# Two cross-attention layers on one core: ScalarE copies the values' bank, and a new order of scores, maxima and turns

## The chip, the core and the metric

The kernel runs on one core of a Trainium2 chip, as one program. The metric is the device time of that core in microseconds (us); the number compared is the median over several runs. A core has TensorE (PE; its weight loads are listed as PEld), VectorE (DVE), ScalarE (ACT), GpSimd (POOL) and SyncE (SP), which here only issues DMAs. The engines run side by side, each works through its own instructions strictly in order, and they meet at semaphores. Matmul results land in PSUM, which has eight banks of 128 partitions by 512 float32.

## The reference

Two cross-attention layers follow each other on x (32 batches, 256 positions, 320 channels; 20 heads of 16). Both attend to one context of 32 x 77 x 512. Layer 0 splits its context into 77 text rows and three more parts, and layer 1 into 77 text rows and a rest; the context has 77 rows, so the text part is all there is, and the other softmaxes are over nothing.

```python
q = _heads(x @ to_q_w)                       # 32 x 20 x 256 x 16
k, v = _heads(ctx @ to_k_w), _heads(ctx @ to_v_w)
s = jnp.einsum('bhqd,bhkd->bhqk', q, k) / np.sqrt(16)
p = jax.nn.softmax(s, axis=-1)               # over 77 keys
out = _merge(jnp.einsum('bhqk,bhkd->bhqd', p, v))
x = out @ to_out_w + to_out_b + x            # then layer 1 in the same way, with its own weights
```

## The kernel before

**Units.** A unit is two batches (one pair `p`) in one layer; 16 pairs and 2 layers make 32 units `u`, in an order that runs layer 0 four pairs ahead of layer 1. x lies as channels by positions: 320 channels are 128 + 128 + 64, and two batches' 64 rest channels share one 128-partition tile. So a unit has five *groups* `g` of 128 channel rows by 256 positions (groups 0 to 3: two channel blocks by two batches; group 4: the rest of both batches). A group holds eight heads, in four pairs, one for each quarter of 32 partitions.

**Steps of a unit.** `queries` or `outputs_and_queries` make the queries, and ScalarE copies them to SBUF. `keys` and `keys_rest` make the keys; ScalarE copies them (`kR`), and GpSimd masks them by head parity (`kT`). `split_keys` and `split_queries` split both on GpSimd into a rounded half and the difference (`k_halves`, `halves`), and DMAs on SP spread these over partitions. `vals` makes the context's values (`psv`), which ScalarE copies to `stage` and a DMA places in `v`. Per group there are then these steps:

- `maxima` (L500, L512): for one *half* of a group (128 positions) four matmuls, one for each quarter of 32 partitions, write scores with positions on partitions into four banks `psm`; two or three halves lie side by side in each bank, and VectorE reduces every bank to row maxima.
- `turn(u)` (L532 to L537), once per unit: VectorE rounds the maxima, subtracts, transposes, and four DMAs on SP lay them as rows into `max_rows`.
- `scores` (L550, L558): four banks `pss`; four matmuls write minus the maxima over all 512 columns, sixteen add the products; ScalarE takes four exponentials to `pT` (L564).
- `values` (L578 to L605): sixteen matmuls write one bank `po` with values and sums (128 x 512); VectorE transposes it in blocks of 32 to `turned` (L590) and takes the reciprocal of the sums (L594); GpSimd multiplies to `normal` (L599).
- `turn_back` (L613): VectorE transposes `normal` into the unit's `oT`, 256 columns per group.
- `finish`, or in a running kernel `outputs_and_queries`: the output matmuls of unit u - 3 (`psy`, from `oT`) and the queries of unit u (`psq`), with VectorE's additions of bias and residual (L620) in between. `main_channels` takes group 0, 1, 2, 3 of `oT` in this order, four matmuls each; the 64-row matmuls that take group 4 come after 64 + 16 others.

**Banks.** All PSUM tiles are one rotating tag of eight banks: every new bank waits until the bank eight allocations before it has been read. The order of the steps thus decides which engine's read a block of matmuls waits for.

**Order.** The framework's scheduler is switched off (`tc.manual_schedule()`). Steps are put by `at(slot, where, step)` into slots, and each slot is issued as written, one kind of step after another. The main part has slots 0 to 134, and four units fill a cycle of 17 slots. By the slot's number in its cycle:

| slot of the cycle | scores | maxima | values | else |
|---|---|---|---|---|
| 0 | 1 group | 3 halves | 1 group | turn, turn back, outputs and queries |
| 1, 2 | 1 | 3 halves | 1 | context values; in 1 keys |
| 3, 4 | 1 | 2 halves | 1 | keys; in 4 turn |
| 5, 9, 13 | 2 groups | none | 1 | outputs and queries |
| 6, 10, 14 | 1 | 3 halves | 2 groups | keys, context values; in 10 and 14 turn |
| 7, 11, 15 | 1 | 3 halves | 1 | two turn backs, keys, mostly context values |
| 8, 12, 16 | 1 | 3 halves | 1 | keys |

The values of a group come one slot after its scores, and groups 0 to 3 are turned back one slot after their values, group 4 in the same slot. Each kind of engine work follows this order, also on VectorE, GpSimd, ScalarE and SP. The order within a slot is

```python
rest = ("values", "rest", "back", "turn", "split", "full", "last")
if slot > 0 and work_of[slot] > 10 * S:
    order = ("load", "scores", "turn back", "maxima") + rest
else:
    order = ("load", "maxima", "turn back", "scores") + rest
```

where `work_of` counts columns of projections and values put into the slot. By it, 88 of the 135 slots have scores first: the output slots (0, 5, 9, 13), the slots with context values, and most of the end. Keys are placed in "rest", outputs and queries in "full", the turn back of group 4 in "back". Of the slots with maxima first, 31 have three halves (slots 1 to 4 of the first cycle, all slots 8, 12 and 16, five slots 2, and slot 113).

Of the kernel before, what the change touches and what calls it, by code (L numbers as in the profile page):

```python
# [52 lines left out]
F32 = mybir.dt.float32  # L53
# [42 lines left out]
def xattn_kernel(ctx: ExitStack, tc: tile.TileContext, xT, cT, cP, weights, outT):  # L96
# [24 lines left out]

    def load_context(u):
        p = units[u][0]
        c_sb = cs[u] = io.tile([P, NKA, NB * L], F32, tag="c", name=f"c_{u}", bufs=3)
        nc.sync.dma_start(out=c_sb, in_=cP[:, p])


# [23 lines left out]

    ones = const.tile([P, P], F32, name="ones")
    nc.vector.memset(ones, 1.0)
    ident = const.tile([P, P], F32, name="ident")
    make_identity(nc, ident)


# [364 lines left out]
    def turn(u):  # L522

        assert u < 2 or (u - 2, NG - 1) in scored
        m = st[u].pop("m").rearrange("p e (g c) j -> p e g (c j)", c=2)
        to = maxes.rearrange("p t y x -> p t (y x)")
        to = to.rearrange("p t (e w g i) -> p t i e g w", e=2, w=8, i=2)
        for t in range(2):
            n = 4 - 3 * t
            new = m[:, :, 4 * t : 4 * t + n]  # L530
            high, low = (to[:, t, i, :, 0:n] for i in range(2))
            nc.vector.tensor_copy(high.bitcast(F32R), new)  # L532
            nc.vector.tensor_tensor(low, new, high, ALU.subtract)  # L533
        mT = work.tile([P, 2 * 4 * 32], F32, tag="mT", name=f"mT_{u}", bufs=1)
        nc.vector.transpose(mT, maxes.rearrange("p t y i -> p (t y i)"))
        for a in range(4):
            nc.sync.dma_start(  # L537
                out=max_rows[u % 2].bitcast(F32).rearrange(
                    "(r x) t (y a n) -> x a r (t y) n", x=4, a=4, n=32
                )[0, a],  # L540
                in_=mT[32 * a : 32 * a + 32].rearrange("r (y n) -> r y n", n=32),
            )


    def scores(u, g):
        scored.add((u, g))
        ps = [bank(f"pss_{u}_{g}_{j}") for j in range(4)]
        for j in range(4):
            r = slice(32 * j, 32 * j + 32)
            nc.tensor.matmul(  # L550
                ps[j][:L], less[r, g % 4, :], max_rows[u % 2][r, g // 4], start=True, stop=False
            )
        for e in range(2):
            q = of_group(st[u]["qs"][:, e], g)
            for half in range(2):
                for j in range(4):
                    r = slice(32 * j, 32 * j + 32)
                    nc.tensor.matmul(  # L558
                        ps[j][:L, e * S : (e + 1) * S], st[u]["ks"][r, e, g, half, :], q[r, :],
                        start=False, stop=(half == 1 and e == 1),  # L560
                    )
        st[u]["p", g] = [probs.tile([P, 512], F32, tag="pT", name=f"pT_{u}_{g}_{j}") for j in range(4)]
        for j in range(4):
            nc.scalar.activation(st[u]["p", g][j][:L], ps[j][:L], AF.Exp, scale=SCALE)  # L564
# [19 lines left out]
                )  # L584
        return po

    def divide(u, g, po):

        turned = work.tile([P, 2 * (S + HD)], F32, tag="turned", name=f"turned_{u}_{g}", bufs=2)
        nc.vector.transpose(turned[:, 0 : 2 * S], po)  # L590

        sums = turned[:, HD : 2 * S - HD].rearrange("p (e n) -> p e n", e=2)[:, :, 0 : S - HD : 32]
        inv = work.tile([P, 2, S // 32], F32, tag="inv", name=f"inv_{u}_{g}", bufs=2)
        nc.vector.reciprocal(inv, sums)  # L594

        outs = turned.rearrange("p (e n) -> p e n", e=2)[:, :, 0:S]
        outs = outs.rearrange("p e (q r) -> p e q r", r=32)[:, :, :, 0:HD]
        normal = work.tile([P, S // 32, 2, HD], F32, tag="normal", name=f"normal_{u}_{g}", bufs=2)
        nc.gpsimd.tensor_tensor(  # L599
            normal.rearrange("p q e d -> p e q d"),  # L600
            outs,
            inv.unsqueeze(3).broadcast_to([P, 2, S // 32, HD]),
            ALU.mult,
        )
        return normal  # L605

    def values(u, g):
        st[u]["n", g] = divide(u, g, products(u, g))

    def turn_back(u, g):  # L610

# [41 lines left out]

    place = {}

    work_of = {}

    def at(slot, where, step, columns=0):

        place.setdefault((slot, where), []).append(step)  # L660
        work_of[slot] = work_of.get(slot, 0) + columns

    def start(u):

# [15 lines left out]
        NU - 2: (end - 2, end - 1, end - 2),  # L680
    }
    made = [0, 0]
    for u, (p, layer) in enumerate(units):

        s = start(u - 2)
        if layer == 0 and u > 0:
            at(s - 5 - (u == 1), "load", lambda p=p: load_x(p))
        if u > 0:
            at(s - 4, "load", lambda u=u: load_context(u))
        if u > 1:  # L690
            k = (0, 1, 2) if u == 2 else (s - 2, s - 1, s + 1)
            at(k[0], "rest", lambda u=u: keys(u, 0), 8 * 2 * L)
            at(k[1], "rest", lambda u=u: keys(u, 1), 8 * 2 * L)
            at(k[2], "rest", lambda u=u: keys_rest(u), 8 * L)
        paired = u > 2 and u - 3 not in late
        if paired:
            at(s, "full", lambda u=u: outputs_and_queries(u - 3, u), 50 * S)
        elif u > 1:
            at(s, "last", lambda u=u: queries(u), 25 * S)
        if u > 1:  # L700
            at(s + 2, "split", lambda u=u: split_keys(u))
            at(start(u - 1), "load", lambda u=u: spread_keys(u))
            for i in range(3):
                at(start(u - 1) + i - 1, "split", lambda u=u, i=i: split_queries(u, i))
                at(start(u - 1) + i, "load", lambda u=u, i=i: spread_queries(u, i))
        need = range(p * NB * L // P, ((p + 1) * NB * L - 1) // P + 1)
        new = [i for i in need if i >= made[layer]]
        made[layer] += len(new)
        first = (-6, -2)[u] if u < 2 else start(u - 1) + 1
        slots = {}  # L710
        for k, i in enumerate(new):
            at(first - 3 - (u == 0) + k, "load", lambda layer=layer, i=i: load_chunk(layer, i))
            if i in few:
                slots[i] = first
                at(first, "full", lambda layer=layer, i=i: vals_of_few(layer, i), 8 * 96)
                continue
            for h in range(2):
                slots[i] = first + (0 if u < 2 else k if len(new) > 1 else h)
                at(slots[i], "full", lambda layer=layer, i=i, h=h: vals(layer, i, h), 4 * C)
        for i in need:  # L720
            at(slots.get(i, first), "full", lambda u=u, i=i: place_vals(u, i))
        for g in range(NG):
            slot = slot_of(u, g)
            at(slot, "scores", lambda u=u, g=g: scores(u, g))
            at(slot + 1, "values", lambda u=u, g=g: values(u, g), 4 * S)
            if g < 4:
                at(slot + 2, "turn back", lambda u=u, g=g: turn_back(u, g))
            else:
                at(slot + 1, "back", lambda u=u, g=g: turn_back(u, g))
        if u == NU - 1:  # L730
            at(end, "full", lambda u=u: finish(u), 20 * S)
            at(end, "last", lambda u=u: finish_rest(u))
        if u in late:
            for t in range(2):
                at(late[u][t], "full", lambda u=u, t=t: finish(u, (t,)), 10 * S)
            at(late[u][2], "rest", lambda u=u: finish_rest(u), 5 * S)
            at(max(late[u]), "last", lambda u=u: store(u))

    groups = [slot_of(u, g) for u in range(NU) for g in range(NG)]
    left = [(u, h) for u in range(3, NU) for h in range(2 * NG)]
    for slot in range(start(1) + 1, end):
# [15 lines left out]
                at(slot, "turn", lambda u=u: turn(u))  # L759
        if parts:  # L760
            at(slot, "maxima", lambda parts=parts: maxima(*parts))


    at(-10, "last", lambda: queries(0))
# [32 lines left out]
    at(3, "load", lambda: load_weights(1, "v", "v", nc.sync))  # L797
    at(4, "load", lambda: load_weights(1, "o", "b", nc.sync))

    rest = ("values", "rest", "back", "turn", "split", "full", "last")  # L800
    for slot in range(min(s for s, _ in place), max(s for s, _ in place) + 1):
        if slot > 0 and work_of[slot] > 10 * S:
            order = ("load", "scores", "turn back", "maxima") + rest
        else:
            order = ("load", "maxima", "turn back", "scores") + rest
        for where in order:
            for step in place.get((slot, where), ()):
                step()
# [98 lines left out]
```

## Time and profile before

| | |
|---|---|
| median of 3 runs | 939.51 us (937.74 to 941.67) |
| the profiled execution | 937.7 us |
| its span, from the first to the last instruction | 935.9 us |
| granted TensorE clock | 0.999 |
| matmuls | 21582, busy 924.1 us |
| VectorE, ScalarE, GpSimd busy | 572.4, 435.9, 413.6 us |
| exponentials (L564), 77 x 512 from PSUM | 640, mean 594 ns |
| transposes of `po` (L590), 128 x 512 from PSUM | 160, mean 689 ns |
| ScalarE copies of 256 columns from PSUM (L421) | 112, mean 373 ns |
| turning back (L613), 128 x 256 | 160, mean 429 ns |
| issues of the turns' DMAs (L537), 32 KB | 128, median 659 ns |

The lines of the profile read so: start in us, duration in us, engine, line of the kernel, operation, output <- inputs, shapes, how many instructions were merged into the line; in square brackets the idle time of that engine just before, and what ended it. "x8" in a merged line is eight instructions, and the duration runs from the start of the first to the end of the last. A weight load (PEld) of a block waits or stands behind waiting matmuls, so the distance between the first weight loads of two blocks is what the block cost TensorE, waits included.

### The profile page before, as it was taken

What the parts mean: (1) busy time and instruction counts of PE and PEld (TensorE: products, weight loads), DVE (VectorE), ACT (ScalarE), POOL (GpSimd) and SP (SyncE); (2) the same over time, 40 slices, a digit from 0 to 9 for tenths busy, and PEclk for the clock granted to TensorE, in tenths of its full rate; (3) what the DMA queues carried; (4) which work ended last, traced back from release to release, by engine and by line L of the source; (5) the groups of instructions that cost most, each with busy time, mean ns of one, the idle gap of its engine ahead of it and who ended that gap; (6) DMA issues with size and microseconds to landing.
All of it is one profiled execution on the core that took longest, in us unless ns stands there. A gap on an engine that the chain in (4) does not pass through costs nothing.

```text
span 935.9 us, 48848 instructions
## 1 busy us (share of the span) xinstructions
PE 924.1 (99%) x21582; PEld 634.5 (68%) x21582; DVE 572.4 (61%) x1324; ACT 435.9 (47%) x975; POOL 413.6 (44%) x614
## 2 busy tenths in 40 slices
PE   9999999999999999999999999999999999999998
PEld 7667766777666777666766667766677766676654
DVE  4485656656566665656556566665467554776575
ACT  2355443554435553454534545434454445444562
POOL 4464334543345543345434455343554335553431
PEclk9999999999999999999999999999999999999999
DMA  6675245352453624545145452354434543344342
GB/s 242 218 225 163 84 132 171 96 191 81 150 178 103 203 67 148 165 142 189 52 140 171 125 184 82 123 171 162 160 95 118 165 158 115 94 141 126 119 137 98
DMA packets 114740, 133.03 MB, mean 142 GB/s; under 512 B 47012, under 2 KB 76004, under 8 KB 114530
## 3 DMA queue, kind: packets, MB, share of 16 engines
q1 hardware_dynamic: 113666, 127.42, 42.8%
q8 instruction: 170, 2.79, 1.3%
q10 hardware_dynamic: 864, 2.49, 0.7%
q14 instruction: 40, 0.33, 0.1%
HBM read 35.39 MB, written 10.49 MB: 49 GB/s over the span
## 4 chain that ended last, share of the span: by engine, by line
PE 88%; DVE 8%; DMA 2%; issue 1%; SPq 0%; POOL 0%; ACT 0%; ACTq 0%; POOLq 0%
PE psq L203 15%; PE psy L203 15%; PE po L578 14%; PE psm L500 8%; PE pss L558 8%; PE psv L203 7%; PE psk L203 6%; PE pss L550 5%; DVE m L512 4%; PE psy L237 4%; PE psq L237 4%; DVE turned L590 2%; PE psk L344 1%; DVE maxes L533 1%; DMA qs<-halves 1%
## 5 line engine op out<-in xcount | busy, mean ns | idle before, releaser
L564 ACT ACTIVATE pT<-pss 77x512 f32<-77x512 f32 x640 | 327.3, 594 | 125.9 <-PE pss L558 120.1
L512 DVE TENSOR_REDUCE m<-psm 128x6 f32<-128x462 f32 (+2 forms) x512 | 247.4, 549 | 208.6 <-PE psm L500 208.1
L599 POOL TENSOR_TENSOR normal<-turned,inv 128x256 f32<-128x256 f32 x160 | 99.5, 622 | 472.5 <-DVE inv L594 452.8
L578 PE MATMUL po<-pT,v 77*32 77x256 f32 x2560 | 165.9, 384 | 4.7 <-DVE m L512 2.7
L203 PE MATMUL psy<-oT,w 128*32 128x256 f32 (+1 forms) x3072 | 164.4, 379 | 0.0
L203 PE MATMUL psq<-x,w 128*32 128x256 f32 (+1 forms) x3072 | 155.6, 380 | 0.5 <-DMA w<-in_w_dram 0.3
L203 PEld LDWEIGHTS psy<-oT,w 128*32 128x32 f32 (+1 forms) x3072 | 88.3, 108 | 63.4 <-issue 14.4
L590 DVE STREAM_TRANSPOSE turned<-po 128x512 f32<-128x512 f32 x160 | 110.3, 689 | 25.6 <-PE po L578 25.5
L203 PEld LDWEIGHTS psq<-x,w 128*32 128x32 f32 (+1 forms) x3072 | 86.0, 109 | 57.7 <-DVE x L620 4.5
L274 POOL TENSOR_SCALAR kT<-kR,masks 128x154 f32<-128x154 f32 x186 | 113.6, 621 | 0.0
L578 PEld LDWEIGHTS po<-pT,v 77*32 77x32 f32 x2560 | 69.6, 109 | 63.4 <-ACT pT L564 18.6
L279 POOL TENSOR_TENSOR halves<-q,halves 128x512 fp32r<-128x512 f32 (+1 forms) x96 | 106.9, 1114 | 8.0
L500 PE MATMUL psm<-kT,q 32*128 32x154 f32 x2560 | 109.4, 296 | 0.0
L558 PE MATMUL pss<-qs,kS 32*77 32x256 f32 x2560 | 106.3, 275 | 0.0
L613 DVE STREAM_TRANSPOSE oT<-normal 128x256 f32<-128x256 f32 x160 | 67.4, 429 | 55.9 <-POOL normal L599 55.9
L620 DVE SCALAR_TENSOR_TENSOR x<-psy,w,x 128x256 f32<-128x256 f32 x160 | 68.4, 476 | 50.7 <-PE psy L203 49.4
L500 PEld LDWEIGHTS psm<-kT,q 32*128 32x128 f32 x2560 | 90.6, 183 | 12.9 <-issue 9.7
L558 PEld LDWEIGHTS pss<-qs,kS 32*77 32x77 f32 x2560 | 88.9, 141 | 10.9
L203 PE MATMUL psv<-w,cv 128*32 128x160 f32 x2432 | 93.2, 299 | 0.2 <-DVE m L512 0.2
L418 ACT COPY q<-psq 128x256 f32<-128x256 f32 x28 | 10.4, 372 | 169.6 <-PE psq L237 169.6
L550 PE MATMUL pss<-max_rows,less 32*77 32x512 f32 x640 | 80.5, 451 | 1.6 <-ACT stage L442 1.6
L203 PEld LDWEIGHTS psv<-w,cv 128*32 128x32 f32 x2432 | 76.8, 110 | 5.2 <-DVE m L512 0.7
(46 smaller groups left out, 725.1 us busy)
## 6 DMA issues: line engine op xcount, KB each, us to landing
qs<-halves SPq DMA_DIRECT2D x256, 128.0 KB
kS<-k_halves SPq DMA_DIRECT2D x128, 192.5 KB
c<-in_cP_dram SPq DMA_DIRECT2D x32, 308.0 KB
cv<-in_cT_dram SPq DMA_DIRECT2D x38, 256.0 KB
out_dram<-x SPq DMA_DIRECT2D x15, 640.0 KB
x<-in_xT_dram SPq DMA_DIRECT2D x14, 640.0 KB
qs<-halves SPq DMA_DIRECT2D x128, 64.0 KB
v<-stage SPq DMA_DIRECT2D x26, 192.5 KB
```

Source lines behind the costliest of these rows:

```text
L203: nc.tensor.matmul(out[m : m + 32], lhsT[:, m : m + 32], rhs, **flags)
L237: nc.tensor.matmul(ps[o : o + 32, 0:S], lhsT, rhs, **flags)
L274: engine.tensor_scalar_mul(kT[:, e], kR[:, groups], masks[:, e : e + 1])
L279: engine.tensor_tensor(low, x, high.bitcast(F32), ALU.subtract)
L500: nc.tensor.matmul(ps[j][:, i * 2 * L : (i + 1) * 2 * L], q[r, c * P : (c + 1) * P], kT[r, :, g % 2, :], start=True, stop=True,)
L512: nc.vector.tensor_reduce(st[u]["m"].rearrange("p e h j -> p h e j")[:, first : first + n, :, j], ps[j][:, at * 2 * L : (at + n) * 2 * L]. ...
L550: nc.tensor.matmul(ps[j][:L], less[r, g % 4, :], max_rows[u % 2][r, g // 4], start=True, stop=False)
L558: nc.tensor.matmul(ps[j][:L, e * S : (e + 1) * S], st[u]["ks"][r, e, g, half, :], q[r, :], start=False, stop=(half == 1 and e == 1),)
L564: nc.scalar.activation(st[u]["p", g][j][:L], ps[j][:L], AF.Exp, scale=SCALE)
L578: nc.tensor.matmul(po[o : o + 32, e * S : (e + 1) * S], vpad[:L, b, pair, e].rearrange("p a d -> p (a d)"), pT[j][:L, e * S : (e + 1) * S] ...
L590: nc.vector.transpose(turned[:, 0 : 2 * S], po)
L599: nc.gpsimd.tensor_tensor(normal.rearrange("p q e d -> p e q d"), outs, inv.unsqueeze(3).broadcast_to([P, 2, S // 32, HD]), ALU.mult,)
```

## The change

- **Copy.** `divide` allocates `whole`, 128 x 512 with two buffers. In slots that are not in `with_outputs`, ScalarE copies the bank `po` to `whole`, and VectorE transposes from there; in `with_outputs` (the output slots and the last nine, 41 groups of 160) VectorE transposes from the bank as before. `normal` is no tile of its own any more but the first half of `whole`.
- **Room.** The context tile has two buffers instead of three, and `ident` takes a buffer of `turned`.
- **Order.** Scores come first in all slots but slot 0 of the kernel and those with exactly two halves of maxima (`fewer`). Where scores come first, the turn back stands behind the maxima instead of ahead of them. The turn stands ahead of the values instead of behind group 4's turn back.
- **Layout of the maxima.** `max_rows` keeps the four quarters' columns together, so the turns' DMAs write runs of 128 elements instead of 32; the matmul that reads them (L550) goes through the rows in the old order, in runs of 32.

```diff
-        c_sb = cs[u] = io.tile([P, NKA, NB * L], F32, tag="c", name=f"c_{u}", bufs=3)
+        c_sb = cs[u] = io.tile([P, NKA, NB * L], F32, tag="c", name=f"c_{u}", bufs=2)
...
-    ident = const.tile([P, P], F32, name="ident")
+    ident = work.tile([P, 2 * (S + HD)], F32, tag="turned", name="ident", bufs=2)[:, 0:P]
...
+        to = max_rows[u % 2].bitcast(F32).rearrange("(r x) t (a n) -> x a r t n", x=4, a=4)[0]
         for a in range(4):
             nc.sync.dma_start(
-                out=max_rows[u % 2].bitcast(F32).rearrange(
-                    "(r x) t (y a n) -> x a r (t y) n", x=4, a=4, n=32
-                )[0, a],
-                in_=mT[32 * a : 32 * a + 32].rearrange("r (y n) -> r y n", n=32),
+                out=to[a], in_=mT[32 * a : 32 * a + 32].rearrange("r (t n) -> r t n", t=2)
             )
...
-                ps[j][:L], less[r, g % 4, :], max_rows[u % 2][r, g // 4], start=True, stop=False
+                ps[j][:L], less[r, g % 4, :],
+                max_rows[u % 2][r, g // 4].rearrange("r (a y n) -> r y a n", a=4, n=32),
+                start=True, stop=False,
...
-    def divide(u, g, po):
+    def divide(u, g, po, direct):
 
         turned = work.tile([P, 2 * (S + HD)], F32, tag="turned", name=f"turned_{u}_{g}", bufs=2)
-        nc.vector.transpose(turned[:, 0 : 2 * S], po)
+        whole = work.tile([P, 2 * S], F32, tag="whole", name=f"whole_{u}_{g}", bufs=2)
+        if direct:
+            nc.vector.transpose(turned[:, 0 : 2 * S], po)
+        else:
+            nc.scalar.copy(whole, po)
+            nc.vector.transpose(turned[:, 0 : 2 * S], whole)
...
-        normal = work.tile([P, S // 32, 2, HD], F32, tag="normal", name=f"normal_{u}_{g}", bufs=2)
+        normal = whole[:, 0:S].rearrange("p (q e d) -> p q e d", e=2, d=HD)
...
-    def values(u, g):
-        st[u]["n", g] = divide(u, g, products(u, g))
+    def values(u, g, slot):
+        st[u]["n", g] = divide(u, g, products(u, g), slot in with_outputs)
...
+    with_outputs = set(range(end - 8, end + 1))
...
         if paired:
-            at(s, "full", lambda u=u: outputs_and_queries(u - 3, u), 50 * S)
+            at(s, "full", lambda u=u: outputs_and_queries(u - 3, u))
+            with_outputs.add(s)
...
+        if len(now) == 2:
+            fewer.add(slot)
...
-    rest = ("values", "rest", "back", "turn", "split", "full", "last")
+    rest = ("turn", "values", "rest", "back", "split", "full", "last")
     for slot in range(min(s for s, _ in place), max(s for s, _ in place) + 1):
-        if slot > 0 and work_of[slot] > 10 * S:
-            order = ("load", "scores", "turn back", "maxima") + rest
+        if slot > 0 and slot not in fewer:
+            order = ("load", "scores", "maxima", "turn back") + rest
```

More of the change, by code (lines that the diff above doesn't have):

```diff
@@ L654, in xattn_kernel, with at @@
     place = {}
-    work_of = {}
-    def at(slot, where, step, columns=0):
+    def at(slot, where, step):
         place.setdefault((slot, where), []).append(step)
-        work_of[slot] = work_of.get(slot, 0) + columns
     def start(u):
@@ L691, in xattn_kernel @@
             k = (0, 1, 2) if u == 2 else (s - 2, s - 1, s + 1)
-            at(k[0], "rest", lambda u=u: keys(u, 0), 8 * 2 * L)
-            at(k[1], "rest", lambda u=u: keys(u, 1), 8 * 2 * L)
-            at(k[2], "rest", lambda u=u: keys_rest(u), 8 * L)
+            at(k[0], "rest", lambda u=u: keys(u, 0))
+            at(k[1], "rest", lambda u=u: keys(u, 1))
+            at(k[2], "rest", lambda u=u: keys_rest(u))
         paired = u > 2 and u - 3 not in late
         if paired:
-            at(s, "full", lambda u=u: outputs_and_queries(u - 3, u), 50 * S)
+            at(s, "full", lambda u=u: outputs_and_queries(u - 3, u))
+            with_outputs.add(s)
         elif u > 1:
-            at(s, "last", lambda u=u: queries(u), 25 * S)
+            at(s, "last", lambda u=u: queries(u))
         if u > 1:
@@ L714, in xattn_kernel @@
                 slots[i] = first
-                at(first, "full", lambda layer=layer, i=i: vals_of_few(layer, i), 8 * 96)
+                at(first, "full", lambda layer=layer, i=i: vals_of_few(layer, i))
                 continue
@@ L718, in xattn_kernel @@
                 slots[i] = first + (0 if u < 2 else k if len(new) > 1 else h)
-                at(slots[i], "full", lambda layer=layer, i=i, h=h: vals(layer, i, h), 4 * C)
+                at(slots[i], "full", lambda layer=layer, i=i, h=h: vals(layer, i, h))
         for i in need:
@@ L724, in xattn_kernel @@
             at(slot, "scores", lambda u=u, g=g: scores(u, g))
-            at(slot + 1, "values", lambda u=u, g=g: values(u, g), 4 * S)
+            at(slot + 1, "values", lambda u=u, g=g, slot=slot: values(u, g, slot + 1))
             if g < 4:
@@ L730, in xattn_kernel @@
         if u == NU - 1:
-            at(end, "full", lambda u=u: finish(u), 20 * S)
+            at(end, "full", lambda u=u: finish(u))
             at(end, "last", lambda u=u: finish_rest(u))
@@ L734, in xattn_kernel @@
             for t in range(2):
-                at(late[u][t], "full", lambda u=u, t=t: finish(u, (t,)), 10 * S)
-            at(late[u][2], "rest", lambda u=u: finish_rest(u), 5 * S)
+                at(late[u][t], "full", lambda u=u, t=t: finish(u, (t,)))
+            at(late[u][2], "rest", lambda u=u: finish_rest(u))
             at(max(late[u]), "last", lambda u=u: store(u))
+    fewer = set()
     groups = [slot_of(u, g) for u in range(NU) for g in range(NG)]
```

## The prediction

> **What bounds the kernel now.** I read the page first, then the waits, then the weight loads (PEld) in order of time, then VectorE (DVE), GpSimd (POOL) and ScalarE (ACT) in the same stretches.
>
> ```profile
> span 935.9 us, 48848 instructions
> PE 924.1 (99%) x21582; PEld 634.5 (68%) x21582; DVE 572.4 (61%) x1324; ACT 435.9 (47%) x975; POOL 413.6 (44%) x614
> PE 88%; DVE 8%; DMA 2%; issue 1%; SPq 0%; POOL 0%; ACT 0%; ACTq 0%; POOLq 0%
> ```
>
> TensorE is busy 99% of the span. The change adds and removes no matmul, so it can only win or lose the waits between blocks, which the weight loads show better than the busy sum. Two neighbouring slots, 33 (16 of its cycle of 17) and 34 (0 of its cycle):
>
> ```profile
> 256.57 0.87 PEld L500 LDWEIGHTS psm<-kT,q 32*128 32x128 f32 x24 [0.25 <-issue]
> 257.34 0.14 PEld L550 LDWEIGHTS pss<-max_rows,less 32*77 32x77 f32 x1
> 257.78 0.15 PEld L550 LDWEIGHTS pss<-max_rows,less 32*77 32x77 f32 x3 [0.30 <-DVE turned L590]
> 258.64 0.59 PEld L578 LDWEIGHTS po<-pT,v 77*32 77x32 f32 x16 [0.17 <-DVE m L512]
> ...
> 260.69 0.15 PEld L550 LDWEIGHTS pss<-max_rows,less 32*77 32x77 f32 x4 [0.24 <-DVE oT L613]
> 261.34 0.85 PEld L500 LDWEIGHTS psm<-kT,q 32*128 32x128 f32 x24
> 262.35 0.59 PEld L578 LDWEIGHTS po<-pT,v 77*32 77x32 f32 x16 [0.17 <-ACT pT L564]
> ```
>
> Slot 33 runs maxima first and takes 2.07 us to the values. Its second score bank is the values' bank of the slot before, eight allocations back, and VectorE frees it late (0.30). Slot 34 runs scores first: 1.66. Over the whole trace the same distance is 1.65 to 1.67 in 49 of 52 slots with scores first and three halves. In the 31 slots with maxima first and three halves it is 1.78 at best and 63.2 us in sum. With two halves, maxima first is the shorter one: 1.45 against 1.66.
>
> VectorE and GpSimd in slot 34:
>
> ```profile
> 262.15 0.45 DVE L613 STREAM_TRANSPOSE oT<-normal 128x256 f32<-128x256 f32 x1 [0.78 <-POOL normal L599]
> 262.52 2.24 DVE L512 TENSOR_REDUCE m<-psm 128x6 f32<-128x462 f32 x4
> 264.68 0.70 DVE L590 STREAM_TRANSPOSE turned<-po 128x512 f32<-128x512 f32 x1
> 266.40 0.45 DVE L613 STREAM_TRANSPOSE oT<-normal 128x256 f32<-128x256 f32 x1 [0.73 <-POOL normal L599]
> 267.04 1.40 DVE L533 TENSOR_TENSOR maxes<-m,maxes 128x64 f32<-128x64 f32 x1
> ```
> ```profile
> 264.08 1.30 POOL L279 TENSOR_TENSOR halves<-q,halves 128x512 fp32r<-128x512 f32 x1
> 267.00 1.30 POOL L279 TENSOR_TENSOR halves<-q,halves 128x512 fp32r<-128x512 f32 x1
> ```
>
> Group 3 is turned back before the reductions, group 4 before the turn; both are inputs of the output matmuls of this slot. The turn's subtraction (L533) takes 1.40 beside a GpSimd operation of 1.30; it has 0.28 in two of its 32 runs and 0.72 in most, always ending 0.13 after GpSimd's operation.
>
> **Part 1, the order of scores and maxima.** All 31 slots go to scores first. At 1.67 each they take 51.8: 63.2 - 51.8 = 11.4 us gained at best. What comes back is a wait of the maxima for banks. In slots 8, 12 and 16 of a cycle the second, third and fourth maxima bank are now those of the values, the keys and the context values of the slot before, all freed by ScalarE. In that slot (7, 11, 15) ScalarE's copy first waits for its buffer: `whole` is also `normal`, with two buffers, so the copy of group 2 waits until group 0 is turned back, and that now stands behind four reductions. Behind the copy wait the key copy, the stage copy and the next four exponentials. The clock, from slots 31 to 33 of the trace: slot 31's turn now starts at 250.81, where GpSimd is idle, so its subtraction takes 0.28 and the turn 1.20 instead of 1.64; two transposes and reciprocals 1.77, to 253.78; reductions to 255.94; group 0 turned back 256.37; copy 256.42 to 257.01 (0.59: 256 columns take 0.37, 512 in an exponential 0.594); key copy to 257.20, stage copy to 257.40. The fourth maxima matmul wants that bank at 256.57 + 0.70 + 0.12 = 257.39. It costs about 0.07 in ten slots: 0.7. After slots 112 and 113, which have little on TensorE, the same chain costs 1.1, in the first slots about 0.8. Part 1: -11.4 + 2.6 = -8.8. If the subtraction stays at 0.72, the chain is 0.44 later: 10 x 0.5 = 5 more; that is the upper end. The lower end is no return, -11.4. I take -8.8, since GpSimd had been idle for 11.8 us before that slot's first `normal`. Two of the 31 also lose a wait of 0.9 to 1.4 for a stage DMA, queued on SP behind the turn's DMAs, which now go out 1.7 sooner; that is within the 11.4. One slot goes from scores to maxima first with two halves: -0.2.
>
> **Part 2, ScalarE's copies.** 119 of 160 groups, 119 x 0.59 = 70 us on an engine that is idle 500 us. The VectorE transposes stay, now from `whole`: at 0.429 for 256 and 0.689 for 512 columns the slope is 1.02 ns, so SBUF saves nothing that these rows show. [...] Its cover is ScalarE's idle time behind the exponentials; where that is gone the copy costs, in slot 4 of a cycle, maxima first after maxima first.
>
> ```profile
> 171.86 2.05 ACT L564 ACTIVATE pT<-pss 77x512 f32<-77x512 f32 x4 [1.16 <-PE pss L558]
> 173.96 0.29 ACT L333 COPY kR<-psk 128x154 f32<-128x154 f32 x1
> ```
>
> The exponentials end late, the copy follows to 174.41, the key copy to 174.60 instead of 174.25; the fourth score matmul at 174.3 needs that bank. +0.3 x 7 = +2.1 (0 to 2.1: in other slots with scores first the copy ends 2 us before the bank is wanted).
>
> **Part 3, turn back behind the maxima, turn ahead of the values, in slot 0 of seven cycles (17 to 119).** From slot 34: maxima end 262.42, reductions 262.43 to 264.67, group 3 back at 265.03. The output matmuls start at 263.24 and need group 3 at their 13th, 12 x 0.0535 later, 263.88: a wait of 1.2. Then the turn: its subtraction meets GpSimd's 1.30 operation and ends with it (turn 2.2), or not (1.3). Transpose to group 4 back takes 264.68 to 266.85 = 2.17. Group 4 is back at 268.8 to 269.5, wanted at 267.67 + 1.2 = 268.87: 0 to 0.6 more. Given back: the query matmuls wait 0.51 and 0.24 for residual additions held up by the turn, and a slot without turn shows none (2.32 from the 64-row outputs to the query's rest, 2.95 here): -0.65. Net 0.5 to 1.15; I take 0.85, since GpSimd's operation lies at that time in both kinds of cycle: 7 x 0.85 = +6.0 (3.6 to 8.0). In the other output slots (5, 9, 13) nothing moves inside, but the group before comes later: I get 0.35 of slack for group 3 and 0.25 for group 4, counted as nothing; without that cover 14 x 0.2 = 3.
>
> **At nothing.** Two context buffers: a load goes out four slots ahead of its use and at least three after the last reader. `ident` is read before the first `turned`. SP: the turn's four DMAs have a median of 0.66 each against about 0.62 for the queries' DMAs with 2 KB runs, so the longer runs save 0.2 per turn, off the path. [...] The matmul that now reads the maxima in runs of 32 elements: no row shows that. The nearest is L500, which reads runs of 77 at its weight loads' pace, so I take nothing; at double time it would be 37 (160 groups, 0.23 on the path for the four matmuls of each), and a gain is excluded, since the old read was one run. [...]
>
> **Sum.** -8.8 - 0.2 + 2.1 + 6.0 = -0.9. The profiled execution took 937.7 (span 935.9 and 1.8 around it), so 936.8; the median of the runs is 1.8 higher, 939.5: I predict 938.6 us. A difference under 0.5% (4.7 us) can hardly be told from none.
>
> **Rivals.** (a) The scores' gain is paid in full and slot 0 keeps only its lower end: -11.4 - 0.2 + 3.6 = -8.0, 931.5 us. For it: nearly all slots with scores first show 1.66 whatever their neighbours; against: there VectorE turned back first. (b) Slower, one mechanism: ScalarE's copy held by the turn back. The place is slots 7, 11 and 15; it decides once group 0 is back later than 256.3 on the clock above, and costs 0.5 in ten slots and about 0.2 in the fourteen output slots that follow: -8.8 + 5.0 + 3.0 + 2.1 - 0.2 + 8.0 = +9.1, 948.6. For it: the margin is 0.01 us, and GpSimd's subtractions already stretch 30 of 32 turns. Against: the turn now precedes the `normal` that it collides with. (c) The read of the maxima in short runs is slow: up to +37, 976. (d) The order changes, and its gain and slot 0's waits cancel: the forecast.
>
> **How the numbers follow.** Forecast (within 4.7 of before) 0.48; (a) 0.25; (b) 0.25; (c) 0.02. The range runs from (a)'s middle to (b)'s, 931.5 to 949.0, and leaves half of each outside at most, and (c); the forecast's own range is 934.8 to 944.2. Faster by over 0.5%: 0.25, same 0.48, slower 0.27.
>
> **What would show it.** Right: 1.66 from first load to values in slots with scores first; in slots 17, 34, 51, ... a wait near 1.2 of `psy` for `oT`, about 12 matmuls in; no wait of `psq` for the additions; L533 at 0.28 in slots 10 and 14. Wrong: `psm` waiting for ScalarE in slots 8, 12, 16 (rival b); no wait for `oT` (rival a); a pss group at L550 longer than 0.46 (rival c).

## The result, and the profile after

The changed kernel takes 943.21 us in the median (942.04 to 946.13, 14 runs), the kernel before, on the same chip, 940.39 (935.89 to 944.23, 14 runs). The ratio is 1.0034, with a 95% interval of 1.0017 to 1.0050: slower, by less than the 0.5% named in the prediction. The forecast of 938.6 lies 4.6 below; its own range (934.8 to 944.2) holds the time, but its sign is wrong. The profiled execution took 942.7 (span 940.9) against 937.7 (935.9), so the two traces differ by 5.0, and it is these 5.0 that are accounted for below. The medians differ by 2.8 only: the profiled execution of before is 2.7 faster than the median of its kernel, that of the changed kernel 0.5.

The page of the changed kernel, the lines that answer to those of before:

```profile
span 940.9 us, 48934 instructions
PE 920.9 (98%) x21582; PEld 634.5 (67%) x21582; DVE 564.5 (60%) x1324; ACT 488.8 (52%) x1094; POOL 413.6 (44%) x614
PE 84%; DVE 5%; POOL 3%; ACT 2%; issue 2%; DMA 2%; SPq 0%; POOLq 0%; ACTq 0%
```

The matmuls are the same in number, their busy time is even 3 less, and the span is longer. ScalarE is busy 53 us more, from the copies (119 of 587 ns, in part side by side with the exponentials ahead of them: the copy at 169.07 begins 0.13 before the fourth exponential ends), and is no bound at 52%. In the chain that ended last GpSimd and ScalarE have gained 5 points together (0% and 0% before), at the cost of TensorE (88%) and VectorE (8%): TensorE now waits for chains that run through them. The view of the waits names the places:

```profile
PEld psy L203 <- DVE oT L618: 24.2, 30, 1.6
ACT whole L594 <- DVE oT L618: 32.2, 21, 2.0
```

The columns are us in total, how often, and the longest. The first is new: output matmuls that wait for groups turned back. The second is ScalarE's copy, held until VectorE has turned back the group that still lies in its buffer.

The weight loads of slots 33 and 34, which the prediction showed of before:

```profile
257.59 0.15 PEld L548 LDWEIGHTS pss<-max_rows,less 32*77 32x77 f32 x4 [0.25 <-issue]
258.24 1.06 PEld L500 LDWEIGHTS psm<-kT,q 32*128 32x128 f32 x24
259.47 0.59 PEld L578 LDWEIGHTS po<-pT,v 77*32 77x32 f32 x16 [0.16 <-issue]
...
261.52 0.15 PEld L548 LDWEIGHTS pss<-max_rows,less 32*77 32x77 f32 x4 [0.24 <-issue]
263.18 0.59 PEld L578 LDWEIGHTS po<-pT,v 77*32 77x32 f32 x16 [0.16 <-ACT pT L564]
263.86 1.21 PEld L203 LDWEIGHTS psy<-oT,w 128*32 128x32 f32 x24
265.96 1.89 PEld L203 LDWEIGHTS psy<-oT,w 128*32 128x32 f32 x40 [0.90 <-DVE oT L618]
267.93 0.78 PEld L237 LDWEIGHTS psy<-oT,w 128*32 128x32 f32 x16
270.20 0.14 PEld L203 LDWEIGHTS psy<-oT,w 64*32 64x32 f32 x5 [1.49 <-DVE oT L618]
272.52 0.59 PEld L237 LDWEIGHTS psq<-x,w 128*32 128x32 f32 x16 [0.41 <-issue]
```

Slot 33 goes from its first load to the values in 259.47 - 257.59 = 1.88, instead of 2.07: better, but not the 1.66 of slot 34, and what is missing stands in one row, the maxima's loads, 1.06 where slot 34 has 0.85 before and 0.84 after. For the outputs of slot 34, the same rows of before:

```profile
263.02 3.37 PEld L203 LDWEIGHTS psy<-oT,w 128*32 128x32 f32 x64
266.48 0.78 PEld L237 LDWEIGHTS psy<-oT,w 128*32 128x32 f32 x16
267.67 0.12 PEld L203 LDWEIGHTS psy<-oT,w 64*32 64x32 f32 x4 [0.41 <-issue]
```

The 64 main loads took 266.48 - 263.02 = 3.46 and now take 267.93 - 263.86 = 4.07, and the step from the next sixteen to the 64-row matmuls takes 270.20 - 267.93 = 2.27 where it took 1.19.

VectorE in the same slot 34, and the GpSimd operation beside its turn:

```profile
263.28 2.28 DVE L512 TENSOR_REDUCE m<-psm 128x6 f32<-128x462 f32 x4 [0.43 <-PE psm L500]
265.48 0.43 DVE L618 STREAM_TRANSPOSE oT<-whole 128x256 f32<-128x256 f32 x1
265.84 1.13 DVE L532 CAST maxes<-m 128x64 fp32r<-128x64 f32 x1
267.00 0.28 DVE L533 TENSOR_TENSOR maxes<-m,maxes 128x64 f32<-128x64 f32 x1
...
268.01 0.67 DVE L592 STREAM_TRANSPOSE turned<-po 128x512 f32<-128x512 f32 x1
269.70 0.45 DVE L618 STREAM_TRANSPOSE oT<-whole 128x256 f32<-128x256 f32 x1 [0.73 <-POOL whole L604]
```
```profile
265.59 1.30 POOL L279 TENSOR_TENSOR halves<-q,halves 128x512 fp32r<-128x512 f32 x1
```

Group 3 is turned back behind the reductions, then comes the turn (265.84 to 268.01, 2.17), and only then the transpose that leads to group 4, which is back at 270.15.

**Where the 5.0 are.** The traces are compared by the distance from the first weight load of one slot's values to that of the next slot's; what a distance has gained or lost is put down to the steps within it. The first four slots differ between executions of the same code by more than the 0.8 in the first row (last section), so that row says little.

| place | after - before, us | foreseen |
|---|---|---|
| first four slots | -0.8 | within part 1 |
| slots 8 and five slots 2 | -0.8 and -0.6 | within part 1 |
| slots 12 and 16, without slot 114 | -3.8 | within part 1 |
| slots 113 and 114 | -0.45 | within part 1 |
| part 1 in sum | -6.5 | -8.8 |
| slot 127, maxima first again | -0.2 | -0.2 |
| outputs of slot 0, seven times | +8.2 | +6.0 |
| slots 4 | +1.6 | +2.1 |
| slots 3, five times 0.46 | +2.3 | 0 |
| outputs of slot 5 in the first cycle | +1.1 | 0 |
| slot 129 | +1.0 | 0 |
| ahead of the values of slots 5, 9 and 13 (-1.2), and a few single places (-1.3) | -2.5 | 0 |
| sum | +5.0 | -0.9 |

### The profile page after: what moved, and what is told of

It is laid out like the page before. It is cut to its first block, busy times and chain, and to the rows that moved or that the text cites. A ratio compares the mean times of both kernels' runs of the same rounds, so it can differ in the third digit from the quotient of the medians.

```text
span 940.9 us, 48934 instructions
## 1 busy us (share of the span) xinstructions
PE 920.9 (98%) x21582; PEld 634.5 (67%) x21582; DVE 564.5 (60%) x1324; ACT 488.8 (52%) x1094; POOL 413.6 (44%) x614
## 2 busy tenths in 40 slices
DMA packets 90166, 133.04 MB, mean 141 GB/s; under 512 B 14245, under 2 KB 51429, under 8 KB 89955
## 4 chain that ended last, share of the span: by engine, by line
PE 84%; DVE 5%; POOL 3%; ACT 2%; issue 2%; DMA 2%; SPq 0%; POOLq 0%; ACTq 0%
PE psq L203 15%; PE po L578 14%; PE psy L203 12%; PE psv L203 8%; PE psm L500 8%; PE pss L558 7%; PE psk L203 6%; PE pss L548 5%; PE psq L237 4%; PE psy L237 3%; DVE m L512 3%; ACT pT L564 2%; PE psk L344 2%; POOL kT L274 1%; DMA v<-stage 1%
## 5 line engine op out<-in xcount | busy, mean ns | idle before, releaser
L604 POOL TENSOR_TENSOR whole<-turned,inv 128x256 f32<-128x256 f32 x160 | 99.5, 622 | 483.7 <-DVE inv L599 439.0
L203 PE MATMUL psy<-oT,w 128*32 128x256 f32 (+1 forms) x3072 | 166.4, 380 | 10.7 <-DVE oT L618 10.6
L203 PE MATMUL psq<-x,w 128*32 128x256 f32 (+1 forms) x3072 | 152.0, 379 | 0.0
L618 DVE STREAM_TRANSPOSE oT<-whole 128x256 f32<-128x256 f32 x160 | 67.4, 433 | 74.7 <-POOL whole L604 74.7
L558 PE MATMUL pss<-qs,kS 32*77 32x256 f32 x2560 | 103.8, 275 | 0.0
L500 PEld LDWEIGHTS psm<-kT,q 32*128 32x128 f32 x2560 | 93.2, 183 | 6.6 <-issue 3.0
L595 DVE STREAM_TRANSPOSE turned<-whole 128x512 f32<-128x512 f32 x119 | 81.0, 681 | 17.3 <-ACT whole L594 17.3
L594 ACT COPY whole<-po 128x512 f32<-128x512 f32 x119 | 67.5, 587 | 32.8 <-DVE oT L618 32.2
```

Of the source, the lines that this page charges most:

```text
L203: nc.tensor.matmul(out[m : m + 32], lhsT[:, m : m + 32], rhs, **flags)
L500: nc.tensor.matmul(ps[j][:, i * 2 * L : (i + 1) * 2 * L], q[r, c * P : (c + 1) * P], kT[r, :, g % 2, :], start=True, stop=True,)
L558: nc.tensor.matmul(ps[j][:L, e * S : (e + 1) * S], st[u]["ks"][r, e, g, half, :], q[r, :], start=False, stop=(half == 1 and e == 1),)
L594: nc.scalar.copy(whole, po)
L595: nc.vector.transpose(turned[:, 0 : 2 * S], whole)
L604: nc.gpsimd.tensor_tensor(normal.rearrange("p q e d -> p e q d"), outs, inv.unsqueeze(3).broadcast_to([P, 2, S // 32, HD]), ALU.mult,)
```

## The experiments

Ten kernels ran. Each was timed against the kernel before in the same rounds; that one had medians of 940.58 (first four), 938.50 (next four) and 939.10 (last two).

**One: both steps of slot 0 back.** In the output slots and the last nine the turn back stands ahead of the maxima again and the turn behind group 4's turn back.

```diff
-    rest = ("turn", "values", "rest", "back", "split", "full", "last")
+    rests = {
+        False: ("turn", "values", "rest", "back", "split", "full", "last"),
+        True: ("values", "rest", "back", "turn", "split", "full", "last"),
+    }
...
+        rest = rests[slot in with_outputs]
...
+            if slot in with_outputs:
+                order = ("load", "scores", "turn back", "maxima") + rest
```

> The changed kernel, but in the output slots (slots 0, 5, 9, 13 of a cycle and the last nine) the turn back stands ahead of the maxima and the turn behind group 4's turn back, as before the change. Theory (VectorE's order in the output slots): the waits of psy for oT in slots 17, 34, ..., 119 go (8.2 us between the traces), and the 1.0 us in slot 129; about 9 us less than the changed kernel: span near 932, ratio to before 0.993 to 0.997. Rival 1 (ScalarE's copies cost it): at most 2 us less, ratio 1.001 to 1.003. Rival 2 (the matmul reads the maxima slower in runs of 32): at most 2 us less.

Measured: 939.30 us, ratio 0.9988 (0.9972 to 1.0004). That is about half of the gain that was expected. Slot 0 costs 0.67 to 0.69 in four cycles and 0.86 to 1.30 in the other three, 5.8 in sum in place of 8.2, and slot 129 nothing in place of 1.0. In slot 34 no `psy` waits for `oT` longer than it did, but the query matmuls wait for the residual additions, first as it was before the change, then here:

```profile
269.66 0.15 PEld L203 LDWEIGHTS psq<-x,w 64*32 64x32 f32 x8 [0.51 <-DVE x L620]
```
```profile
270.97 0.15 PEld L203 LDWEIGHTS psq<-x,w 64*32 64x32 f32 x8 [1.18 <-DVE x L625]
```

The old order in slot 0 does not bring the old slot 0 back, because its inputs come later. Slot 33 now runs its maxima behind its scores, so its reductions end later, and the transpose of its values stands behind them: VectorE begins to turn group 3 back at 263.46, 2.12 after the first load of slot 34 (261.34), where it was 1.46 (260.69 to 262.15). Everything behind it on VectorE, the turn and the additions too, is that much later.

**Two: the turn late, alone.** As the first, without the last two lines of its diff.

> The changed kernel, but in the output slots the turn alone is behind group 4's turn back again; the turn back stays behind the maxima. Theory: the first wait of psy for oT stays at about 1.2 from the 13th matmul on, the second (1.08) goes, the additions are held up by the turn again but after a wait that hides it: 0.5 us less per slot, 7 x 0.5 + 1.0 = 4.5 us less than the changed kernel, span near 936.5, ratio to before 0.997 to 1.001. Rival 1 and 2: no more than 1 us less, ratio 1.002 to 1.004.

Measured: 936.21, ratio 0.9966 (0.9951 to 0.9982): faster than before, and some 6.5 less than the changed kernel where 4.5 were expected. Slot 0 costs 0.27 to 0.30 in four cycles and 0.46 to 0.91 in the other three, 3.1 in sum; in slot 34:

```profile
266.07 1.88 PEld L203 LDWEIGHTS psy<-oT,w 128*32 128x32 f32 x40 [0.90 <-DVE oT L618]
269.23 0.12 PEld L203 LDWEIGHTS psy<-oT,w 64*32 64x32 f32 x4 [0.41 <-issue]
270.88 0.23 PEld L203 LDWEIGHTS psq<-x,w 64*32 64x32 f32 x8 [0.17 <-DVE x L625]
```

The first wait, group 3 behind the reductions, is as in the changed kernel. The second is gone (0.41 is what these loads show in the kernel before, too), so it came from the turn. The waits for the additions have nearly gone as well: VectorE reduces while GpSimd makes `normal`, where in the first experiment it stood idle 0.80 for it.

**Three: the turn back ahead, alone.** The last two lines of the first diff, without the rest.

> The changed kernel, but in the output slots the turn back alone is ahead of the maxima again; the turn stays ahead of the values. Theory: no first wait, but group 4 comes only 0.36 sooner, so the second wait takes most of what the first one gave: 7 x 0.36 = 2.5 us less than the changed kernel, span near 938.4, ratio 0.999 to 1.003. If the first wait of 1.2 were the cost by itself, 8 us less. Rival 1 and 2: unchanged, ratio 1.002 to 1.005.

Measured: 943.13, ratio 1.0032 (1.0014 to 1.0050), as the changed kernel (the profiled execution, 947.4, is a long one: its first four slots took 4.8 more than the changed kernel's). Slot 0 still costs 1.06 to 1.27 in six cycles and 1.77 in the seventh; the 2.5 us that were expected from it did not come. So of the two steps moved in slot 0 the turn is the one that costs, 5.2 of the 8.2 with the turn back behind the maxima (experiment two), 2.7 with it ahead (experiments one and three); the wait for group 3 is absorbed by the wait for group 4 behind it. The 3.1 that are left with the turn late are not the place of the turn back, since with that put back as well slot 0 costs 5.8.

**Four: without ScalarE's copies.** VectorE transposes all 160 groups from the bank; all else is the changed kernel.

```diff
-        st[u]["n", g] = divide(u, g, products(u, g), slot in with_outputs)
+        st[u]["n", g] = divide(u, g, products(u, g), True)
```

> The changed kernel without ScalarE's copies: VectorE transposes from the bank in all slots; the orders, the layout of the maxima and the shared buffers stay. Theory: the copy held behind the turn back costs only 0.2 us in ten slots and about 0.1 in slots 4 of a cycle, and VectorE frees the values' bank 0.3 later than ScalarE did there: -3 to +1 us against the changed kernel, ratio 1.000 to 1.005. Rival 1 (ScalarE's copies are the cost): 4 us or more less, ratio below 0.999. The other way round (the copies are what makes scores first pay): 5 us or more longer, ratio above 1.008.

Measured: 968.37, ratio 1.0309 (1.0283 to 1.0334): 25 us slower than with the copies, far from the theory and the way that was named as the other one (the copies are what makes scores first pay). In slot 32 of it, a slot 15 of its cycle:

```profile
260.69 0.67 PEld L500 LDWEIGHTS psm<-kT,q 32*128 32x128 f32 x6
261.93 0.82 PEld L500 LDWEIGHTS psm<-kT,q 32*128 32x128 f32 x18 [0.56 <-DVE turned L592]
```

With scores first the second maxima bank is the values' bank of the slot before. VectorE frees it only behind the reductions of that slot, here behind its turn as well, and the maxima wait. Against the kernel before, slots 11 and 15 lose up to 1.2 by it, slots 0 and most slots 3 0.5 to 0.7, and the output slots 5, 9 and 13, whose scores wait in the same way, 0.4 to 0.5 each (slot 5 of the first cycle 1.5).

**Five: the order alone.** Only the rule for scores first, in the kernel before; its turn back, turn and layout stay.

```diff
-        if slot > 0 and work_of[slot] > 10 * S:
+        if slot > 0 and slot not in fewer:
```

> The kernel before with one part of the change: scores first in all slots but those with two halves of maxima. No copy, the turn back ahead of the maxima and the turn late, as before. Theory (scores first needs the values' bank sooner than VectorE frees it): 15 to 25 us longer than before, ratio 1.016 to 1.027, with the waits in the slots after 8, 12, 16 and in 11 and 15, as without the copy in e4. Rival (the order pays by itself): 5 to 11 us less, ratio 0.988 to 0.995.

Measured: 950.82, ratio 1.0108 (1.0073 to 1.0143): 12 us longer, the way of the theory and less than its 15 to 25. The same wait of the maxima for `turned`, now 0.26 in slot 33 and 0.23 in slot 34. Slots 9, 13 and 0, whose order the rule does not touch, lose 0.2, 0.4 and 0.5 each: slots 8, 12 and 16, now with scores first, hand their reductions on late. Of the 14.8 between the traces, 3.5 stand in slots 63 and 64 alone, where the maxima wait 3.00 for a stage copy.

**Six: the copies alone.** The copies with their buffers, in the kernel before: the parts Copy and Room of the change, line for line.

> The kernel before with ScalarE's copies alone (and the shared buffers that make room), in the slots in which the changed kernel has them; all orders as before. Theory: the waits of the scores for the values' bank in slots 12 and 16 go (0.3 to 0.4 us in seven to ten slots), and in slots 4 the key copy is late by 0.1 to 0.6 us: -3 to +1 us, ratio 0.996 to 1.001. Rival 1 (ScalarE's copies cost by themselves): 4 us or more longer, ratio above 1.004.

Measured: 947.32, ratio 1.0087 (1.0061 to 1.0112), slower than the theory, and where the rival (the copies cost by themselves) has it. Its slot 0 shows why; the first row is VectorE, the second a weight load:

```profile
264.10 0.71 DVE L595 STREAM_TRANSPOSE turned<-whole 128x512 f32<-128x512 f32 x1 [0.36 <-ACT whole L594]
```
```profile
273.39 0.15 PEld L203 LDWEIGHTS psq<-x,w 64*32 64x32 f32 x8 [1.08 <-DVE x L625]
```

ScalarE's copy stands behind the four exponentials of its slot. So VectorE, strictly in order, waits for it and hands the delay on: it begins to turn group 3 back 2.03 after the slot's first load (263.86 to 265.89) where it was 1.46, the turn and the additions follow, and the queries wait. That is +3.9 in the outputs of slot 0. Five slots 3 lose 0.4 each (+2.0), slots 4 together +1.9, slot 114 +1.6, the first four slots, which vary, +2.3, and all other places together gain 1.8. On the banks the copies give next to nothing in this order. In slot 33 the scores no longer wait for the values' bank (0.30 before), but the values wait for the reductions instead, 0.43 where it was 0.17, and the slot is as long as before:

```profile
261.81 0.59 PEld L578 LDWEIGHTS po<-pT,v 77*32 77x32 f32 x16 [0.43 <-DVE m L512]
```

Alone the order costs 1.1% and the copies 0.9%; if the two were independent, both would cost 2.0%, and with the early turn (5.6 us by the second experiment's trace) more. Together they cost 0.34% with the early turn and gain 0.34% with the turn late in the output slots. These two kernels also have the turn back behind the maxima, the turn ahead of the values in the other slots, and the layout, so the difference is not the pair's alone; experiment four, one edit away from the changed kernel, shows the pair without these.

**Seven: the layout alone.** The new order of `max_rows`, the DMAs' runs of 128 and the matmul's read in runs of 32, in the kernel before.

> The kernel before with the new layout of max_rows alone: DMA runs of 512 bytes, the matmul reads in runs of 32 elements. Theory (both are off the path; the matmuls' rate is unchanged): 0 to 2 us less, ratio 0.997 to 1.001; L550 at the same 0.23 us from its first load to that of L558. Rival 2 (the read in short runs is slow): 3 us or more longer, ratio above 1.003.

Measured: 939.18, ratio 1.0010 (0.9993 to 1.0027): no difference. The loads of that matmul take 139 ns in the mean in the kernel before (L550), here (L548) and in the changed kernel (L548).

**Eight: the turn behind the outputs.** The first experiment, with the turn of an output slot moved behind the output and query matmuls and their additions.

```diff
-        True: ("values", "rest", "back", "turn", "split", "full", "last"),
+        True: ("values", "rest", "back", "split", "full", "turn", "last"),
```

> As e1 (turn back ahead of the maxima in the output slots), with the turn behind the output and query steps there, so that VectorE's residual additions come before it. In e1 the query matmuls of slot 34 waited 1.18 + 0.24 us for the additions, which stood behind the turn; before the change it was 0.51 + 0.24. Theory: that wait goes, and slot 0's stretch is 0.67 us shorter than before the change instead of 0.67 longer: 7 x 1.35 = 9.4 us less than e1, span near 928, ratio to before 0.987 to 0.992. Rival (the additions are late for another reason, such as the reductions that start later): as e1, ratio 0.997 to 1.000.

Measured: 930.32, ratio 0.9903 (0.9882 to 0.9925), faster than both kernels and as expected. Slot 0 gains 0.5 to 0.6 in six cycles and nothing in the seventh, in place of losing 1.05 to 1.76; in slot 34:

```profile
262.62 3.37 PEld L203 LDWEIGHTS psy<-oT,w 128*32 128x32 f32 x64
269.58 0.59 PEld L237 LDWEIGHTS psq<-x,w 128*32 128x32 f32 x16 [0.41 <-issue]
```
```profile
267.97 2.16 DVE L625 SCALAR_TENSOR_TENSOR x<-psy,w,x 128x256 f32<-128x256 f32 x5 [0.85 <-PE psy L203]
270.04 0.22 DVE L532 CAST maxes<-m 128x64 fp32r<-128x64 f32 x1
270.30 0.28 DVE L533 TENSOR_TENSOR maxes<-m,maxes 128x64 f32<-128x64 f32 x1
```

No wait inside the main loads; the additions wait for TensorE and not the reverse; and the turn, behind them, meets no GpSimd operation, so its subtraction takes 0.28.

**Nine: a third buffer for `whole`.** In the changed kernel, nothing else.

```diff
-        whole = work.tile([P, 2 * S], F32, tag="whole", name=f"whole_{u}_{g}", bufs=2)
+        whole = work.tile([P, 2 * S], F32, tag="whole", name=f"whole_{u}_{g}", bufs=3)
```

> The changed kernel with three buffers for whole instead of two; nothing else. Theory (the held copy, rival b, at a tenth of its size): the maxima of slots 8, 12 and 16 wait 0.22 in ten slots because ScalarE's copy of group 2 stands idle 1.61 for the turn back of group 0, with the key and stage copies behind it. With a third buffer the copy starts at once: 0.2 gone in ten slots, -2.0 against the changed kernel, span near 939, ratio near 1.001 to the kernel before. Slot 0 keeps its +1.1. Other theory (the maxima wait for the exponentials or the stage copy itself, not for the buffer): nothing moves, ratio 1.003 to 1.004.

Measured: 940.77, ratio 1.0011 (0.9997 to 1.0026). The interval still touches that of the changed kernel, so here the trace decides. ScalarE in slot 33, in the changed kernel and then here, and the weight loads here:

```profile
257.47 0.59 ACT L594 COPY whole<-po 128x512 f32<-128x512 f32 x1 [1.61 <-DVE oT L618]
```
```profile
257.75 0.59 ACT L594 COPY whole<-po 128x512 f32<-128x512 f32 x1
258.66 0.29 ACT L333 COPY kR<-psk 128x154 f32<-128x154 f32 x1 [0.32 <-PE psk L203]
```
```profile
260.26 0.84 PEld L500 LDWEIGHTS psm<-kT,q 32*128 32x128 f32 x24
261.27 0.59 PEld L578 LDWEIGHTS po<-pT,v 77*32 77x32 f32 x16 [0.17 <-ACT pT L564]
```

The copy follows its exponentials at once, where it had stood idle 1.61 for the turn back; the maxima's loads take 0.84 again. Slots 12 and 16 get 0.2 shorter in eleven cases, slot 114 by 1.2, in sum 3.5, for the 2.0 that were expected. The span does not show it (940.7), mainly since the first four slots of this execution were 2.7 longer.

**Ten: all of it.** The eighth experiment with the third buffer, maxima first also in a slot ahead of one with two halves, and no copy in the slots 2 and 3.

```diff
-        st[u]["n", g] = divide(u, g, products(u, g), slot in with_outputs)
+        st[u]["n", g] = divide(u, g, products(u, g), slot in with_outputs or slot + 1 in fewer)
...
-        if slot > 0 and slot not in fewer:
+        first = slot > 0 and slot not in fewer and (slot + 1 not in fewer or slot > end - 9)
+        if first:
```

> The kernel with the turn behind the output matmuls, and three further edits: a third buffer for whole, maxima first in a slot that stands ahead of one with two halves (the slots 2 of a cycle), and VectorE's transposition straight from the bank, without ScalarE's copy, in slots that stand ahead of one with two halves (2 and 3 of a cycle). Theory by intervals: slots 3 lose their wait of 0.46 and slots 2 give back 0.13, in five cycles -1.65; slots 4 lose 0.12 six times and 0.59 and 0.37, -1.7; slots 12 and 16 lose 0.2 ten times, -2.0. Sum -5.3: span 923, ratio near 0.985. Rival: the bank's late release by VectorE in slots 2 and 3 comes back as a wait of the scores, as in the kernel without copies (0.3 to 0.7 in fourteen slots), and takes it back: ratio 0.990 or above.

Measured: 924.95, ratio 0.9851 (0.9825 to 0.9877), span 923.2, the fastest kernel here. By intervals against the eighth: slots 3 -2.3 and slots 2 +0.9, slots 4 -1.8, slots 12 and 16 -3.3 (1.2 of it in slot 114, not counted on), and +1.3 in the intervals of slots 1 and 5, not foreseen; in sum -5.2, near the -5.3 expected, though in part by other terms. In the chain that ended last TensorE has 96%, and no other engine more than 1%.

## Why the prediction was right or wrong

**The sum.** It gave -0.9, and the traces give +5.0. The 5.9 between them are slot 0, priced too low (2.2), the return on part 1, priced too low (2.3), slots 3, counted at nothing (2.3), and two single places, counted at nothing (2.1); slots 4 take 0.5 off, and gains that the sum does not have 2.5. That the time still lies within the forecast's own range is owed to these last 2.5: without them it would have been near 945.7.

**Slot 0: right place, wrong end of the range.** The first step that failed is the price of part 3, "I take 0.85". All its parts were there; the clock ran near its upper case, 1.15 a slot, and 1.05 to 1.11 were measured in six slots. The turn was priced at 2.2 if it meets GpSimd's 1.30 operation and 1.3 if not, and the middle was taken although the operation lies there in both kinds of cycle. In all seven slots it was met, in six by the cast ahead of the subtraction, in one by the subtraction. The seventh slot cost 1.76, since there the old turn had been one of the two that met nothing, so nothing was given back. Experiments two and three show that of the two steps moved it is the turn that costs: with it late, 3.1 of the 8.2 are left.

**Slot 0: a miscount that cancelled.** The wait for group 3 was given as 1.2, by 12 matmuls of 0.0535. But the profile records two matmuls for each output matmul that is written (64 main ones for 32 in the code; the values' sixteen records are eight in the code too, while the scores' matmuls stand once each), and the account of the kernel ahead of the prediction counts both ways: "four matmuls each" for a group are statements, "64 + 16 others" are records. So group 3 is wanted at the 25th record, 1.28 after the first. By the prediction's own clock the wait is 265.03 - 264.52 = 0.51, and 0.61 was measured (4.07 - 3.46). The row said so: the loads break after "x24". It did no harm to the sum, because group 4 comes back at a time that does not depend on it: what the first wait lacked, the second got. That the sum came out near is luck there.

**The additions: right.** The queries' rest follows 2.32 after the 64-row outputs, as foreseen (272.52 - 270.20), and gives 0.63 back in slot 34.

**Part 1: right mechanism, one term too small.** Slots 8, 2, 113 and the stage DMAs (slots 50 and 63, together -2.6) went as said; L533 has 0.28 in slots 10 and 14. The clock of the held copy was right to 0.03: the stage copy was to end 0.83 after slot 33's first load and ended 0.85 after it (258.44 - 257.59). What failed, the second step, is the price of being just late: "about 0.07 in ten slots" was 0.22 (1.06 - 0.84). That is 1.5 of the 2.3 that part 1 lacks. Experiment nine shows the cause, the buffer that `whole` and `normal` share. It is rival b's mechanism, priced at 0.5 there. The other 0.8 was not taken apart.

**Part 2: the copy's cover was sought on the wrong engine.** Slots 4 came at +1.6 for +2.1. But the part, the third step that failed, looked only at ScalarE, whose idle time hides the copies, and left out that VectorE's transpose now starts behind the exponentials, and its reductions and turn backs with it. That is part of the +2.3 of slots 3, where the values wait for the reductions:

```profile
286.93 0.59 PEld L578 LDWEIGHTS po<-pT,v 77*32 77x32 f32 x16 [0.64 <-DVE m L512]
```

In the sixth experiment, with the old order, the same slots lose 0.4, also behind the reductions; in the fifth, without copies, they lose 0.36, there as a wait of the scores for the values' bank (0.30 in slot 37), which VectorE comes to 0.42 later in slot 36 than before, behind later reductions. Either edit alone does it, and both together do little more. The sum also never asked what the order would cost without the copies. It was silently credited with banks "all freed by ScalarE"; that credit is worth 25 us in the changed kernel (experiment four).

**Counted at nothing.** The other output slots held their cover: after the first cycle the intervals with their outputs are as long as before to 0.02, but for one of +0.3 and two of -0.3. Two single places did not: the outputs of slot 5 in the first cycle (+1.1) and slot 129 (+1.0), where the last turn, moved ahead of the values, holds up the transpose and the addition that free two banks for the scores (waits of 0.40 and 0.47). Experiments one and two have slot 129 at 0.0, so the turn's place is its cause; the first outputs stay at +0.9 to +1.1 in experiments one to three, and their cause was not separated. The layout and its strided read were rightly counted at nothing (experiment seven), and rival c is out. In neither trace does a weight load wait for a context load (the DMAs that weight loads wait for are those of `w` alone, 0.6 us before and 0.8 after), so the context tile's two buffers show no cost either. With the longer runs the profile's packets under 512 bytes fell from 47012 to 14245, and the turn's DMAs have a median of 629 ns (L538) where they had 659, so about 0.12 per turn for the 0.2 that was foreseen. In experiment seven, with this layout alone, it makes no difference in the time (939.18 against 938.50), and in neither trace does a weight load wait for these DMAs. What does wait, in slots 50 and 63, is a stage copy for a DMA queued on SP behind them, and there the layout alone gained 0.3 and 0.0.

## What to carry to other kernels

Where engines work in order and share banks, an early read of a bank on an idle engine and an order that wants the bank early are one edit (here 1.0108 and 1.0087 alone, 1.0034 in the changed kernel, which has both): price the pair, and follow the delay of the copy along the engine that waits for it, not along the one that makes it. A step that nobody waits for, as this turn, belongs behind the work that somebody waits for: its place behind the outputs instead of ahead of them was worth 8 to 9 us between experiments one and eight (ratios 0.9988 and 0.9903, spans 937.5 and 928.4). And where a range's ends are "meets the other engine" and "does not", look up in the trace which of them happens at that place, and count the records, not the statements.

## What had not been expected of the hardware

- The stretching beside GpSimd is not tied to the two-input subtraction. With the turn moved, the subtraction (L533) has 0.28 to 0.29 in 31 of 32 turns and 16.1 us in sum, where it had 33.1; but in six turns the cast ahead of it (L532, one input) takes 1.11 to 1.14 beside GpSimd's 1.30 operation, where it takes 0.18 to 0.30 in all others but one. In slot 34 it ends 0.08 after that operation (266.97 and 266.89).
- The VectorE transposes of 128 x 512 take 681 ns in the mean from SBUF (119) and 700 from PSUM (41) in the changed kernel, 689 from PSUM before: 8 and 19 ns less from SBUF, where the prediction's rows had shown no saving.
- A bank that comes free just after it is wanted can cost more than it is late. In slot 33 the stage copy frees the fourth maxima bank at 258.44, 0.08 after the matmuls of the other three began (258.36), and the maxima's loads take 0.22 longer (1.06, with a third buffer 0.84).
- The first four slots, the same code in experiments one to three, differ by up to 4.5 us between executions (-0.5, +0.2 and +3.9 against before).
